# Four reorderings in a four-layer graph transformer: first weight between the first rows, expert loads prepared one ahead, first queries inside the graph stage, a token sum pinned

## The chip, the cores and the metric

The kernel runs on one core of one Trainium2 chip. The metric is the device time of one execution in microseconds, the median over several runs. Engines: PE (TensorE, matrix products and transposes), DVE (VectorE), ACT (ScalarE), POOL (GpSimd), and SP (SyncE), which issues most of the DMAs. Every engine works through its own instructions in a fixed order; an instruction that waits holds up all that stand behind it on that engine.

## The reference

The input is x with 1250 tokens of 512 features and 20,000 edges (src, dst) between tokens. Four layers follow each other, each of this form:

```python
xn = layernorm(x)
x = x + gnn(xn, edges) + mixer(xn)
x = x + ffn(layernorm(x))
```

What the change touches of them:

- Layer 0: the graph part is `relu` of a normalised neighbour sum of `xn @ W + b`; the mixer is a two-block performer attention, which begins with its own layer norm of xn with gain and bias, projects keys and values, and uses exponentials of `key @ projection` less half the key's squared norm.
- Layer 1: the graph part is `relu(batchnorm(mean_of_neighbours @ W_l + b_l + xn @ W_r))`; the mixer is a linear attention with a softmax over each query's features.
- Layer 2's feed-forward part: 8 experts, 2 per token, each `h1 = rmsnorm(gelu(x @ w1))`, `h2 = rmsnorm(gelu(h1 @ w2))`, output `(h1 + h2) @ w3`, summed with the gates' weights.
- Layer 3: the graph part is a `leaky_relu` of a normalised neighbour sum; the mixer is `mean(X @ Wv) + X @ kv / (n sqrt(d))` with `kv = (X @ Wtheta)^T (X @ Wv)`, where the mean is over all tokens.

## The kernel before, in words

The tokens lie in 10 tiles of 125 (NT = 10, TP = 125), the features in 4 chunks of 128 (NC = 4). `nat` tiles have tokens on partitions; `xnT` has features on partitions and all 1250 tokens in a row. Products are in float32 and pass through PE twice, so that one `mm` of four chunks over a 125-token tile is eight passes. Eight PSUM banks are handed out by `bank()`. Three weight buffers are handed out by `load_w` (L156), whose DMA goes on SP's queue. A planner in the framework (the tile scheduler) orders the instructions of each engine by their costs and dependencies, not by the order of the source; only what is wrapped in `tc.keep_in_program_order` keeps its place among the other wrapped instructions and what they stand behind.

*Opening, `layer0_mixers` and `l0_front`.* SP's queue starts with cols (per-feature biases and gains), then x in five loads of two tiles each, then the graph weight W. Per tile `ln_one` computes the layer norm on DVE (`bn_stats` L194, `bn_aggr` L196, a square root on ACT, a reciprocal L199, the scaling L200), z is a second normalisation of xn (L790), both are transposed on PE (L188); xn's transposed copy goes to xnTt by ACT, z's to `yT` (the same memory as `xnT`) with gain and bias from cols by DVE and ACT (L735). The product with W for tile t-1 stands in the source behind the preparation of tile t; its bias is added by DVE (L798) into hs.

*The graph's counting matrix, `Graph`.* In DRAM lies adj, 1250 x 1250 counts. `__init__` makes a tile of zeros out of x's last tiles (L555, DVE) and writes it over adj and a part of yd by DMAs on POOL's queue. `start` makes a key per edge, transposes the keys on PE (L584) and copies them (L585). `add` handles ten columns of edges: a load of the keys along a row (keyrow, two buffers, SP's queue), ten comparisons with every key (`same`, L614, DVE), then L617 and L618 on DVE and ten scatter-additions into adj by POOL (L620). There are 16 such groups, called between other work of layer 0.

*Layer 0's attention, `l0_attention`.* For one of four feature chunks `keys` runs the key projection (`proj_T`, three column blocks, evicted by DVE with bias into kT, L831), its square on ACT (L865), the squared sums on PE against `halves`, and then the products with the projection pj; `values` (L849) follow. At the end the output bias is added tile by tile to the residual (L1040, DVE, on `xm`, which is `xn` here).

*Layer 1.* `LinearAttention` (used as `att`) has `q_start`: a product with wq, a maximum (L1278), a subtraction (L1280), an exponential on ACT, a sum (L1285), a reciprocal (L1286) and a product (L1287). `out` calls it for the tiles 0 and 1, then per tile turns q (L188), starts the query two tiles on, and multiplies with `mix`. Ahead of it the graph part runs a loop over four features f (L1441 to L1452): eight products per column block, an Identity activation with bias into hT, batch statistics, a square root on ACT, four small DVE steps and a Relu with scale. hT is transposed back (L1462) tile by tile behind the attention's output.

*Layer 2's experts, `second` and `third`.* Sorted token rows are worked on in loads of one or two tiles of 128 rows. Per load, `second` loads w2, scales h1 by its root mean square (L1657, DVE) and transposes it (L1659, PE), evicts it with the gain n1 into h1T (L1702, DVE), multiplies with w2 and applies gelu on ACT (L1708). `third` does the same with h2 and n2, adds h1T (sT, L1724, DVE), multiplies with w3 and hands the result to `put`. Each load's chain stands in the source, and on PE, in this order: transposes, then products.

*Layer 3.* Each arriving tile of xn is transposed into xnT (ACT, L1772) and added to a Gram matrix (L1774). Then `graph(0)`, four products of the Gram matrix with wv whose results are copied into half (L145, by ACT and DVE in turn), the token sum tot over xnT (L1813, DVE), its spread totb (L1815, DVE), the product of totb with wv, whose result is added to x (`add_row` on POOL), and `graph(1)` follow, and then the products of half with wt.

Of the kernel before, what the change touches and what calls it, by code (L numbers as in the profile page):

```python
# [8 lines left out]
F32 = mybir.dt.float32  # L9
# [48 lines left out]
def gps_d4_kernel(ctx: ExitStack, tc: tile.TileContext, a: dict, out: bass.AP):  # L58
# [19 lines left out]
        for r in (slice(0, 112), slice(112, TP)):  # L78
            engine.dma_start(o[r], i[r])

    def load_x(engine, o):
        for t in range(0, NT, 2):
            move(engine, o[:, t:t + 2, :], a["x"][t * TP:(t + 2) * TP, :].rearrange("(t p) d -> p t d", p=TP))

    cols = const.tile([P, NCOL], F32, name="cols")
    nc.sync.dma_start(cols, a["cols"])
    ident = const.tile([P, P], F32, name="ident")
    make_identity(nc, ident)
    ones = const.tile([P, P], F32, name="ones")
# [98 lines left out]
            nc.tensor.transpose(ps[:, tok(c)], src[:, fea(c)], ident[:TP, :TP])  # L188
        return ps[:, :NC * TP].rearrange("p (c t) -> p c t", t=TP)

    def ln_one(o, src, t, between=lambda: None):

        st = S.small.tile([TP, 6], F32, tag="st1", name="st1", bufs=4)
        nc.vector.bn_stats(st, src[:, t, :])  # L194
        mv = S.small.tile([TP, 4], F32, tag="mv1", name="mv1", bufs=4)
        nc.vector.bn_aggr(mv[:, 0:2], st)  # L196
        nc.scalar.activation(mv[:, 2:3], mv[:, 1:2], AF.Sqrt, bias=eps5[:TP])
        between()
        nc.vector.reciprocal(mv[:, 2:3], mv[:, 2:3])  # L199
        nc.vector.tensor_scalar(o, src[:, t, :], mv[:, 0:1], mv[:, 2:3], op0=OP.subtract, op1=OP.mult)  # L200
        return mv
# [344 lines left out]
    class Graph:  # L546
# [1 line left out]

        def __init__(self, pool, first, x):
            self.pool = pool
            self.next = 0

            nc.vector.tensor_scalar(first, x[:, 7:, :].rearrange("p t d -> p (t d)")[:, :T], 3e38, 0.0,  # L555
                                    op0=OP.is_gt, op1=OP.is_lt)
            for t in range(NT):
                move(nc.gpsimd, adj[t * TP * T:(t + 1) * TP * T, :].rearrange("(p d) o -> p (d o)", d=T), first)
            nc.gpsimd.dma_start(adj[T * T:T * T + TP, :], first[:, 0:1])
            n = RARE * SL // 8  # L560
            for k in range(8):
                r = (NTI - RARE) * SL + k * n
                nc.gpsimd.dma_start(yd[r:r + n, :], first[:n, :D])
            self.count = pool.tile([TP, EC], F32, name="count")
            self.cell = pool.tile([TP, EC], I32, name="cell")

        def start(self, z):

# [202 lines left out]
                assert self.turned < self.rooted  # L771
                self.some()

    def l0_front(pool, x0, xn, hs):


        w = load_w(a["L0_gnn_W"])
        b = row_bc(a["L0_gnn_b"])
        yT = xnT
        before = None  # L780
        for t in range(NT + 1):
            if t < NT:
                mv = ln_one(xn[:, t, :], x0, t)
                r = S.small.tile([TP, 2], F32, tag="r2", name="r2", bufs=4)

                nc.vector.tensor_tensor(r[:, 0:1], mv[:, 2:3], mv[:, 2:3], op=OP.mult)
                nc.scalar.activation(r[:, 1:2], mv[:, 1:2], AF.Sqrt, bias=eps5[:TP], scale=r[:, 0:1])
                nc.vector.reciprocal(r[:, 1:2], r[:, 1:2])
                z = S.small.tile([TP, D], F32, tag="z", name="z")
                nc.vector.tensor_scalar(z, xn[:, t, :], r[:, 1:2], None, op0=OP.mult)  # L790
                xnTt = S.small.tile([P, NC, TP], F32, tag="xnTt", name="xnTt")
                nc.scalar.copy(xnTt, transposed(xn[:, t, :]))
                gained(yT, t, transposed(z), ("L0_mix_ln1_g", "L0_mix_ln1_b", 0))
            if before is not None:
                u, m = before
                ps = bank()
                mm(ps[:TP, :], [(m[:, c, :], w[:, c, :]) for c in range(NC)])
                nc.vector.tensor_tensor(hs[:, u, :], ps[:TP, :], b[:TP, :], op=OP.add)  # L798
            before = t, xnTt
        return yT, z  # L800

    def l0_gnn(rows, dis, hs, xn):
# [318 lines left out]
    def layer0_mixers():  # L1121
# [3 lines left out]
        with tc.tile_pool(name="l0a", bufs=1) as pool:  # L1125
            xn = nat(pool, "xn")
            hs = nat(pool, "hs")
            with tc.tile_pool(name="l0n", bufs=1) as lp:
                x0 = nat(lp, "x0")
                load_x(nc.sync, x0)  # L1130
                zero = lp.tile([TP, T], F32, name="zero")
                graph = Graph(gpool, zero, x0)
                yT, z = l0_front(pool, x0, xn, hs)
                graph.start(z)
            second = [Front(yT, xn, ("L0_mix_ln2_g", "L0_mix_ln2_b", 4 * i)) for i in range(2)]
            first = Front(yT, xn, ("L0_mix_ln1_g", "L0_mix_ln1_b", 4))
# [127 lines left out]
    class LinearAttention:  # L1264
# [22 lines left out]
            nc.vector.tensor_tensor(q, q, bc(m, C), op=OP.mult)  # L1287
            return q

        def out(self, pool, wq, use):  # L1290


            ready = [self.q_start(pool, t, wq) for t in range(2)]
            for t in range(NT):
                qT = pool.tile([P, NC, TP], F32, tag="qT", name="qT", bufs=3)
                nc.scalar.copy(qT, transposed(ready[t].rearrange("p h c -> p (h c)")))
                if t + 2 < NT:
                    ready.append(self.q_start(pool, t + 2, wq))
                ps = bank()
                mm(ps[:TP, :], [(qT[:, c, :], self.mix[:, c, :]) for c in range(NC)])  # L1300
                use(t, ps[:TP, :])
# [80 lines left out]
    def layer1_mixers():  # L1382
        scales = dram.tile([T, 1], F32, name="scales")
        with tc.tile_pool(name="l1x", bufs=1) as pool:
# [46 lines left out]
                add_to(mT[:, f, c0:c0 + cn], ps)  # L1431

            over(rows, False, more)
            hT = pool.tile([P, NC, T], F32, tag="n1", name="hT")
            for f in range(NC):
                st = S.small.tile([P, 5, 6], F32, tag="bst", name="bst")
                for c0, cn in CH:
                    ps = bank()
# [11 lines left out]
                nc.vector.tensor_tensor(g[:, 1:2], mv[:, 0:1], g[:, 0:1], op=OP.mult)  # L1450
                nc.vector.tensor_tensor(g[:, 1:2], col("L1_gnn_beta", f), g[:, 1:2], op=OP.subtract)
                nc.scalar.activation(hT[:, f, :], hT[:, f, :], AF.Relu, bias=g[:, 1:2], scale=g[:, 0:1])  # L1452
            rscope.close()

            b = row_bc(a["L1_mix_b_out"], late=True)
            ow = row_bc(a["L1_mix_out_norm_w"], late=True)
# [30 lines left out]
                return gT  # L1487

            arrival[1] = Arrival(1, a["L1_ffn_gw2"], hidden=hidden)
            with tc.tile_pool(name="l1o", bufs=1) as op:  # L1490
                att.out(op, wq, use)
                arrival[1].step(NT)

    def layer1_ffn():
        KH = 8
# [114 lines left out]
    def layer2_ffn():  # L1610
# [4 lines left out]
        with tc.tile_pool(name="l2o", bufs=1) as op:  # L1615
# [29 lines left out]
            with tc.tile_pool(name="l2e", bufs=1) as pool:  # L1645
# [16 lines left out]
                class Group:  # L1662
# [8 lines left out]
                    def first(self, source):  # L1671
# [15 lines left out]
                            o += n  # L1687
                        self.r1 = self.means(ss[:, :self.n], "r1")

                    def second(self):  # L1690
                        self.h1T = pool.tile([P, 2, GT * SL], F32, tag="h1T", name="h1T", bufs=2)
                        self.h2 = pool.tile([SL, GT, DH], F32, tag="h2", name="h2", bufs=2)
                        ss = pool.tile([SL, GT], F32, tag="s2", name="s2", bufs=2)
                        for i, (o, tiles) in zip(self.loads, self.at):
                            n = len(tiles)
                            e = expert(i)
                            w2 = op.tile([P, 2, DH], F32, tag="w2", name="w2", bufs=4)
                            nc.sync.dma_start(w2, a["L2_ffn_w2"][bass.ds(e, 1), :, :].rearrange("o (c p) h -> p (o c) h", p=P))
                            n1 = cols_of(e, "L2_ffn_n1", "n1")
                            pt = turned(self.h1, self.r1, o, n)  # L1700
                            for k in range(2):
                                nc.vector.tensor_scalar(self.h1T[:, k, o * SL:(o + n) * SL], pt[:, k, :], n1[:, k:k + 1], None,  # L1702
                                                        op0=OP.mult)
                            ps = bank()
                            for j in range(n):
                                mm(ps[:, j * DH:(j + 1) * DH],
                                   [(self.h1T[:, k, (o + j) * SL:(o + j + 1) * SL], w2[:, k, :]) for k in range(2)])
                            nc.scalar.activation(self.h2[:, o:o + n, :], ps[:, :n * DH].rearrange("p (j d) -> p j d", d=DH),  # L1708
                                                 AF.Gelu)
                            for j in range(o, o + n):  # L1710
                                square(self.h2[:, j, :], ss[:, j:j + 1])
                        self.r2 = self.means(ss[:, :self.n], "r2")

                    def third(self):
                        for i, (o, tiles) in zip(self.loads, self.at):
                            n = len(tiles)
                            e = expert(i)
                            w3 = half3().rearrange("p (c n) -> p c n", c=2)
# [4 lines left out]
                            for k in range(2):  # L1723
                                nc.vector.scalar_tensor_tensor(sT[:, k, :n * SL], pt[:, k, :], n2[:, k:k + 1],  # L1724
                                                               self.h1T[:, k, o * SL:(o + n) * SL], op0=OP.mult, op1=OP.add)
                            for j, t in enumerate(tiles):
                                ps = bank()
                                mm(ps, [(sT[:, k, j * SL:(j + 1) * SL], w3[:, k, :]) for k in range(2)])
                                put(pool, ps, t)

                def use(loads, source):
                    n = len(loads)
# [14 lines left out]
    def layer3_mixers():  # L1747

        with tc.tile_pool(name="l3a", bufs=1) as pool:
# [60 lines left out]
                copy(half[:, c, :], ps)  # L1810

            tot = S.small.tile([P, NC], F32, tag="tot", name="tot", bufs=1)
            nc.vector.tensor_reduce(tot, xnT, AX.X, OP.add)  # L1813
            totb = S.small.tile([P, NC, TP], F32, tag="totb", name="totb", bufs=1)
            nc.vector.tensor_scalar(totb, bc(tot, TP), 1.0 / T, None, op0=OP.mult)  # L1815
            ps = bank()
# [104 lines left out]
```

## Time and profile before

| | before |
|---|---|
| median of 9 runs | 3118.08 us (3110.11 to 3131.32) |
| the profiled execution | 3121.38 us |
| its span | 3119.4 us |
| mean granted clock of TensorE | 0.958 |
| DMA traffic | 275.69 MB, mean 88 GB/s |

The tables below are from that one execution; times are microseconds from the start of its span. A row of the timeline gives the start, the duration, engine, line, operation, what is written and read, the shape, the count of merged instructions, and in brackets the idle time of the engine ahead of it with what ended it ("<-DVE q L1287": VectorE's instruction on line 1287 that writes q). In such a row `x8` from a PE line are eight passes. "PEq" is PE's own instruction sequencer. The page's slices cut the span into 40 equal parts and give the busy share of each in tenths.

Busy time by stage (PE and DVE in us):

| stretch | length | PE | DVE | DMA share | granted clock | what it holds |
|---|---|---|---|---|---|---|
| 0 to 20 | 20.00 | 6.09 | 14.31 | 0.95 | 1.00 | loads, first layer norms |
| 20 to 61.5 | 41.50 | 41.50 | 19.84 | 0.86 | 1.00 | layer 0's product with W |
| 61.5 to 135 | 73.50 | 73.19 | 66.38 | 0.58 | 0.98 | layer 0's first key and value projections |
| 1726 to 1745 | 19.00 | 16.10 | 9.70 | 0.08 | 0.91 | layer 1's last batch norm, first queries |
| 2606 to 2718 | 112.00 | 94.75 | 49.67 | 0.50 | 1.00 | layer 2's experts, second and third products |
| 2786 to 2835 | 49.00 | 45.65 | 20.47 | 0.01 | 1.00 | layer 3's Gram matrix and token sum |

A granted clock below 1 in a stretch means that the throttle held PE at half speed for a part of it.

### The profile page before, as it was taken

The numbers are of one execution on the slowest core, as the hardware profiler recorded it, in microseconds if no ns is written. First come the engines' busy times: TensorE is split into PE (matmuls) and PEld (weight loads), VectorE is DVE, ScalarE is ACT, GpSimd is POOL, SyncE is SP. The second block draws the span as 40 slices with busy tenths as digits, with TensorE's granted clock in tenths as the row PEclk, the third lists the DMA queues.
The fourth block names the chain that finished last, engine by engine and source line by source line (L and its number), as shares of the span: only waits on it lengthen the run. The fifth ranks groups of instructions, "written<-read, shape, count | busy, mean of one in ns | idle before, by whom it ended". The sixth has DMA issues, their size and how long they took to land. (4 is left out here: it accounts for less than half of the span.)

```text
span 3119.4 us, 31412 instructions
## 1 busy us (share of the span) xinstructions
PE 2877.0 (92%) x11531; PEld 1720.4 (55%) x11531; DVE 1178.2 (38%) x2812; ACT 694.0 (22%) x1469; POOL 670.7 (22%) x492
## 2 busy tenths in 40 slices
PE   8999999999999999999899979999799979789884
PEld 4457744455576444655455546766454547345562
DVE  6835611143365423344531550001343135362433
ACT  3132311132333122111311431111241013230010
POOL 3444444442001300133310011000301002032023
PEclk9999999999999999999899989999899989999987
DMA  8411121121001200237310017775210026430096
GB/s 230 118 15 15 7 38 31 28 32 14 14 14 46 76 27 28 80 113 246 88 34 1 21 48 280 257 251 176 81 41 1 8 70 194 160 106 10 24 319 195
DMA packets 234381, 275.69 MB, mean 88 GB/s; under 512 B 104351, under 2 KB 131599, under 8 KB 234209
## 3 DMA queue, kind: packets, MB, share of 16 engines
q1 hardware_dynamic: 123841, 185.13, 18.5%
q0 software_dynamic: 96832, 63.67, 9.0%
q10 hardware_dynamic: 13536, 24.65, 2.1%
q8 instruction: 102, 1.67, 0.2%
q14 instruction: 70, 0.57, 0.1%
HBM read 228.04 MB, written 44.91 MB: 88 GB/s over the span
## 5 line engine op out<-in xcount | busy, mean ns | idle before, releaser
L182 PE MATMUL ps<-xnT,w 128*128 128x500 f32 (+1 forms) x1536 | 554.5, 515 | 2.8 <-PEq L698 2.2
L182 PE MATMUL ps<-w,hT 128*125 128x512 f32 (+1 forms) x1232 | 542.1, 592 | 0.7 <-ACT hT L1246 0.7
L182 PEld LDWEIGHTS ps<-xnT,w 128*128 128x128 f32 x1536 | 289.2, 190 | 251.8 <-issue 239.4
L620 POOL DMA_INDIRECT adj<-count,cell x160 | 318.3, 1990 | 369.0 <-DMA adj<-count,cell 345.7
L182 PEld LDWEIGHTS ps<-w,hT 128*125 128x125 f32 (+1 forms) x1232 | 228.8, 189 | 270.2 <-issue 261.1
L182 PE MATMUL ps<-w,xnT 128*125 128x512 f32 x560 | 254.7, 604 | 0.0
L182 PE MATMUL ps<-xgT,w 128*128 128x256 f32 (+1 forms) x1256 | 233.4, 344 | 2.8 <-issue 2.0
L182 PEld LDWEIGHTS ps<-xgT,w 128*128 128x128 f32 x1256 | 207.1, 193 | 43.3 <-issue 20.7
L378 POOL DMA_INDIRECT xg<-rows,r_idx x94 | 89.8, 955 | 571.1 <-PE ps L419 288.4
L208 DVE TENSOR_TENSOR xn<-ps,xn 125x512 f32<-125x512 f32 x100 | 69.0, 690 | 344.0 <-PE ps L182 344.0
L523 ACT ACTIVATE hT<-ps,cols 128x500 f32<-128x500 f32 (+1 forms) x108 | 65.6, 608 | 477.3 <-PE ps L182 477.3
L439 POOL DMA_INDIRECT came<-yd,slots x80 | 102.9, 1286 | 300.5 <-SPq L408 136.3
L182 PEld LDWEIGHTS ps<-w,xnT 128*125 128x125 f32 x560 | 103.6, 192 | 115.4 <-issue 115.0
L420 DVE COPY xgT<-ps 128x512 f32<-128x512 f32 x94 | 62.0, 687 | 246.3 <-PE ps L419 225.3
L182 PE MATMUL ps<-hs,AT 125*125 125x512 bf16 x600 | 132.6, 379 | 4.0 <-PEq L698 4.0
L182 PE MATMUL ps<-AT,n 125*128 125x500 bf16 (+1 forms) x720 | 127.2, 339 | 0.0
L429 DVE TENSOR_TENSOR y<-ps,erow 128x512 f32<-128x512 f32 x71 | 49.1, 692 | 194.4 <-PE ps L182 188.4
L182 PEld LDWEIGHTS <-AT 125*125 125x125 bf16 x600 | 81.3, 136 | 50.7 <-issue 6.1
L1532 ACT ACTIVATE hT<-ps,b 128x256 f32<-128x256 f32 (+1 forms) x112 | 48.8, 436 | 262.1 <-PE ps L182 262.1
L182 PEld LDWEIGHTS <-n 125*128 125x128 bf16 x720 | 70.0, 97 | 58.0 <-issue 1.1
L925 PE MATMUL ps<-ex,vw 125*65 125x256 f32 x320 | 83.6, 413 | 2.8 <-DVE vw L911 2.8
L208 DVE TENSOR_TENSOR x<-ps,x 125x512 f32<-125x512 f32 x50 | 34.5, 690 | 130.1 <-PE ps L182 116.8
(404 smaller groups left out, 3644.8 us busy)
## 6 DMA issues: line engine op xcount, KB each, us to landing
w<-in_L_ffn_we_dram SPq DMA_DIRECT2D x56, 1024.0 KB
w<-in_L_ffn_w_dram SPq DMA_DIRECT2D x58, 512.0 KB
yd<-y ACTq DMA_DIRECT2D x94, 256.0 KB
w<-in_L_mix_W_dram SPq DMA_DIRECT2D x16, 1024.0 KB
w<-in_L_ffn_w_dram SPq DMA_DIRECT2D x44, 256.0 KB
rows<-z SPq DMA_DIRECT2D x40, 224.0 KB
keyrow<-keys SPq DMA_DIRECT2D x16, 546.9 KB
erow<-in_L_ffn_b_dram SPq DMA_DIRECT2D x30, 256.0 KB
```

Source lines behind the costliest of these rows:

```text
L182: nc.tensor.matmul(o, l, r, start=(i == 0), stop=(i == n - 1))
L208: nc.vector.tensor_tensor(dst, ps, dst, op=OP.add)
L378: nc.gpsimd.indirect_dma_start(g, None, self.rows, bass.IndirectOffsetOnAxis(ap=self.idx[:, t:t + 1], axis=0))
L420: nc.vector.tensor_copy(xgT[:, :, j * SL:(j + 1) * SL], ps.rearrange("p (c s) -> p c s", c=NC))
L429: nc.vector.tensor_tensor(y, ps, bias, op=OP.add)
L439: nc.gpsimd.indirect_dma_start(y, None, yd, bass.IndirectOffsetOnAxis(ap=slots[n][:, k * NT + t:k * NT + t + 1], axis=0))
L523: nc.scalar.activation(hT[:, f, :cn], ps[:, :cn], act, bias=b1(f))
L620: nc.gpsimd.indirect_dma_start(adj, bass.IndirectOffsetOnAxis(ap=self.cell[:, c:c + 1], axis=0), self.count[:, c:c + 1], None, compute_op= ...
L925: nc.tensor.matmul(self.ps[j][:C + 1, :NB], self.vw[j][:, t, :], self.ex[k][:, j, u, :], start=(t == 0), stop=(t == NT - 1))
L1532: nc.scalar.activation(hT[f // NC][:, f % NC, :ns], ps[:, :ns], AF.Gelu, bias=b1[:, f:f + 1])
```

## The change

Four places, independent of each other:

1. Opening. x's first two tiles are loaded singly, W's load follows them, then tiles 2 and 3, then cols, then the rest of x. The zero fill and the clearing DMAs move out of `Graph.__init__` into `clear`, which `l0_front` calls at its seventh tile; the zero fill is pinned in program order, and so is the `bn_stats` of tile 2. The product with W lags two tiles behind the preparation instead of one, and xnTt has three buffers of a pool of its own.
2. Layer 2's experts. `second` and `third` are cut into `prepare` (weight load, scaling, transposes, eviction) and `use` (products and what follows), and a new method `ahead` issues the next load's `prepare` before this load's `use`.
3. Layer 1. The first two `q_start` calls are made ahead of the last of the four features of the batch-normed graph part; for that the attention's pool is opened, and the graph part's closed, before that loop.
4. Layer 3. The token sum's reduction is pinned in program order.

The diff, cut to its core:

```diff
-    def load_x(engine, o):
-        for t in range(0, NT, 2):
-            move(engine, o[:, t:t + 2, :], a["x"][t * TP:(t + 2) * TP, :].rearrange("(t p) d -> p t d", p=TP))
+    def load_x(engine, o, tiles=range(0, NT, 2), n=2):
+        for t in tiles:
+            move(engine, o[:, t:t + n, :], a["x"][t * TP:(t + n) * TP, :].rearrange("(t p) d -> p t d", p=TP))
...
-    nc.sync.dma_start(cols, a["cols"])
...
-    def ln_one(o, src, t, between=lambda: None):
+    def ln_one(o, src, t, between=lambda: None, in_order=False):
-        nc.vector.bn_stats(st, src[:, t, :])
+        ins = nc.vector.bn_stats(st, src[:, t, :])
+        if in_order:
+            tc.keep_in_program_order(ins)
...
-        def __init__(self, pool, first, x):
+        def __init__(self, pool):
...
-            nc.vector.tensor_scalar(first, x[:, 7:, :].rearrange("p t d -> p (t d)")[:, :T], 3e38, 0.0,
-                                    op0=OP.is_gt, op1=OP.is_lt)
+        def clear(self, first, x):
+            tc.keep_in_program_order(nc.vector.tensor_scalar(first, x[:, 7:, :].rearrange("p t d -> p (t d)")[:, :T], 3e38, 0.0,
+                                    op0=OP.is_gt, op1=OP.is_lt))
             for t in range(NT):
                 move(nc.gpsimd, adj[t * TP * T:(t + 1) * TP * T, :].rearrange("(p d) o -> p (d o)", d=T), first)
...
-    def l0_front(pool, x0, xn, hs):
-        w = load_w(a["L0_gnn_W"])
+    def l0_front(pool, x0, xn, hs, w, aside):
...
-        before = None
-        for t in range(NT + 1):
+        before = []
+        for t in range(NT + 2):
+            if t == 6:
+                aside()
             if t < NT:
-                mv = ln_one(xn[:, t, :], x0, t)
+                mv = ln_one(xn[:, t, :], x0, t, in_order=t == 2)
...
-                xnTt = S.small.tile([P, NC, TP], F32, tag="xnTt", name="xnTt")
+                xnTt = pool.tile([P, NC, TP], F32, tag="xnTt", name="xnTt", bufs=3)
...
-            if before is not None:
-                u, m = before
+            if t > 1:
+                u, m = before[t - 2]
...
-                load_x(nc.sync, x0)
+                load_x(nc.sync, x0, range(2), 1)
+                w = load_w(a["L0_gnn_W"])
+                load_x(nc.sync, x0, range(2, 4, 2))
+                nc.sync.dma_start(cols, a["cols"])
+                load_x(nc.sync, x0, range(4, NT, 2))
                 zero = lp.tile([TP, T], F32, name="zero")
-                graph = Graph(gpool, zero, x0)
-                yT, z = l0_front(pool, x0, xn, hs)
+                graph = Graph(gpool)
+                yT, z = l0_front(lp, x0, xn, hs, w, lambda: graph.clear(zero, x0))
...
-        def out(self, pool, wq, use):
-            ready = [self.q_start(pool, t, wq) for t in range(2)]
+        def first(self, pool, wq):
+            return [self.q_start(pool, t, wq) for t in range(2)]
+        def out(self, pool, wq, use, ready=None):
+            ready = ready or self.first(pool, wq)
...
             over(rows, False, more)
+            rscope.close()
+            oscope = ExitStack()
+            op = oscope.enter_context(tc.tile_pool(name="l1o", bufs=1))
             hT = pool.tile([P, NC, T], F32, tag="n1", name="hT")
             for f in range(NC):
+                if f + 1 == NC:
+                    ready = att.first(op, wq)
...
+                    def ahead(self, prepare, use):
+                        loads = [(i, *at) for i, at in zip(self.loads, self.at)]
+                        made = prepare(*loads[0])
+                        for k, load in enumerate(loads):
+                            now, made = made, prepare(*loads[k + 1]) if k + 1 < len(loads) else None
+                            use(*load, now)
...
-                        for i, (o, tiles) in zip(self.loads, self.at):
+                        def prepare(i, o, tiles):
...
+                            return w2
+                        def use(i, o, tiles, w2):
...
+                        self.ahead(prepare, use)
...
-            nc.vector.tensor_reduce(tot, xnT, AX.X, OP.add)
+            tc.keep_in_program_order(nc.vector.tensor_reduce(tot, xnT, AX.X, OP.add))
```

## The prediction

> **What bounds the kernel now.** I read the page from the top: the busy shares first, then the slices.
>
> ```profile
> PE 2877.0 (92%) x11531; PEld 1720.4 (55%) x11531; DVE 1178.2 (38%) x2812; ACT 694.0 (22%) x1469; POOL 670.7 (22%) x492
> ...
> PE   8999999999999999999899979999799979789884
> ...
> DVE  6835611143365423344531550001343135362433
> ```
>
> TensorE (PE) is busy 92% of the 3119.4 us span, in all stages but a few slices. So an edit is worth the PE idle time that it takes away or opens in its own stage, plus what the clock loses behind that idle time. I therefore went to the timeline of PE at the four places that the change touches, with VectorE (DVE) beside it. I also followed the order of instructions that the changed program has on each engine, because in all but the pinned places a scheduler decides that order.
>
> **The opening.** First PE, then DVE, before:
>
> ```profile
> 17.74 6.30 PE L182 MATMUL ps<-w,xnTt 128*125 128x512 f32 x8 [3.98 <-DMA w<-in_L_gnn_W_dram]
> ...
> 61.64 0.34 PE L584 MATMUL ps<-ident,kf 80*125 80x80 f32 x2
> 61.82 8.60 PE L182 MATMUL ps<-xnT,w 128*128 128x500 f32 x24
> 70.26 1.80 PE L182 MATMUL ps<-halves,sq 128*125 128x2 f32 x16
> ```
>
> ```profile
> 62.45 0.31 DVE L585 COPY key<-ps 125x160 f32<-125x160 f32 x1
> ...
> 63.02 0.34 DVE L614 SCALAR_TENSOR_TENSOR same<-keyrow,key,mask 125x125 f32<-125x125 f32 x1
> ...
> 65.71 0.74 DVE L831 TENSOR_SCALAR kT<-ps,cols 128x500 f32<-128x500 f32 x1
> ```
>
> PE waits 3.98 us for the first weight, then has no gap over 0.3 us until 135. The front end ends at 61.8 (call this E), the key projection takes 8.60, and at 70.26 the squared-key sums follow, which need kT by way of DVE's L831 and one ACT square (0.62 us).
>
> *Loads.* The weight now stands behind two tiles instead of ten. That could remove the 3.98 us, but two other things take its place. The changed PE order has the transposes of three tiles, not two, ahead of the first product. And DVE's four biased transposed copies (L735) of the first two tiles need cols, which landed at 2.95 and now stands behind 1 MB of x and the 1 MB weight. The x pairs (0.5 MB each) landed at 5.7, 7.77, 9.96, 12.21 and 14.69, so about 2.3 us per 0.5 MB: the 2 MB ahead of cols land at about 5.7 + 3 x 2.3 = 12.6, and cols at about 13. Tile 2's statistics, 0.53 + 0.48 of xn and z and its transposes (1.04 each, at the half clock) then end about 16 to 18.7. Against 17.74 that is -1.7 to +1; the 4.29 us per tile afterwards is PE's own. The zero fill (0.79 us) and the 42.8 us of clearing (18.63 to 61.45) start about 20 us later; the first scatter waits anyway, since POOL's first one had stood idle 242 us for x. I take **-0.3**.
>
> *What becomes late.* DVE is in order. Before, 10 comparisons (L614) stood between the key copy and the first kT eviction. In the changed order 60 do, with ten residual adds (L1040), five L617 and five L618. From start to start a comparison takes 0.27 us (63.28, 63.55, 63.83 in the trace), an add about 0.65 (0.68 long, starts 0.60 to 0.74 apart), an L617 and L618 together about 0.2. The first eviction then stands at 62.45 + 0.57 + 60 x 0.27 + 10 x 0.65 + 5 x 0.2 = 86.7 instead of 65.71: 21 us later. The projection's PSUM space suffices, so PE still ends it at E + 8.6; the sums start at 86.7 + 0.74 + 0.62 + 0.3 = 88.4, not 70.26. PE's order has nothing between: **18 us**, the lower end. The key rows come through two buffers by DMA, and the longest time from issue to use was 5.9 us (65.83 to 71.73). The first two groups of ten are loaded; four more at a round of (5.9 + 2.7)/2 = 4.3 end at 63.0 + 5.4 + 17.2 = 85.6 without the adds; the adds and the L617 and L618, if none lies in those waits, make it 93: 24 us. The late clearing shares the queues, hence an upper end of 26. I take **21**, and +1 (0 to 2) for a half-clock start behind the stall. Nothing is paid back: DVE's later load is smaller, but PE waited nowhere for it.
>
> **Layer 2's experts.** Between 2606 and 2718 PE has 28 gaps over 0.3 us, all of 0.44 to 1.05 us, 17.25 us together, of this kind:
>
> ```profile
> 2608.99 0.70 PE L182 MATMUL ps<-w,h1T 128*128 128x256 f32 x2 [0.58 <-DVE h1T L1702]
> ...
> 2688.05 3.70 PE L182 MATMUL ps<-w,sT 128*128 128x512 f32 x8 [0.58 <-DVE sT L1724]
> ```
>
> Each is four transposes, then DVE's normalising eviction (0.88 for two), then the product. The changed PE order puts the next load's transposes ahead of this load's products, whose 1.2 to 3.6 us cover the 0.88. What stays is the first load of each call (some four times 0.6) or, at worst, gaps where DVE's 1.66 us runs of L1657 stand ahead of the eviction (10 x 0.6). **-15** (-17 to -11).
>
> **Layer 1's queries.** Before:
>
> ```profile
> 1725.65 7.03 PE L182 MATMUL ps<-w,xnT 128*125 128x512 f32 x16
> 1735.58 0.62 PE L188 MATMUL ps<-ident,q 125*128 125x125 f32 x4 [2.90 <-DVE q L1287]
> 1736.03 5.30 PE L182 MATMUL ps<-w,xnT 128*125 128x512 f32 x8
> 1741.16 3.60 PE L182 MATMUL ps<-mix,qT 128*125 128x512 f32 x8
> ```
>
> PE waits 2.90 us for the softmax of the first queries, and then runs 5.30 for eight passes that take 3.60 two lines on: the granted clock was half until 1739.94. Moved ahead of the last feature's matmuls, the two softmaxes have some 20 us. New on the path is that feature's batch norm: 0.47 + 0.42 + 0.29, a table load of 1.28 (one of two that ACT gains), 0.29, four small DVE steps of 0.2 and a Relu of 1.43, together 5.0 to 5.4, against PE work of 0.43 + 3.43 + 3.43 = 7.3 before the first hT transpose. It is covered by 1.9; uncovered, a second table load would eat it. -2.90 - 1.7 = **-4.6** (-5 to -2.5).
>
> [...]
>
> **Layer 3's token sum.** Before, DVE then PE:
>
> ```profile
> 2794.03 5.36 DVE L1813 TENSOR_REDUCE tot<-xnT 128x4 f32<-128x5000 f32 x1 [1.00 <-ACT xnT L1772]
> ...
> 2826.70 0.69 DVE L145 COPY half<-ps 128x512 f32<-128x512 f32 x1 [6.17 <-PE ps L182]
> ```
>
> ```profile
> 2806.26 6.66 PE L182 MATMUL ps<-hs,AT 125*125 125x512 bf16 x30 [3.35 <-PEq L698]
> 2812.76 13.90 PE L182 MATMUL ps<-w,gram 128*128 128x512 f32 x32
> 2826.50 3.60 PE L182 MATMUL ps<-w,totb 128*125 128x512 f32 x8
> ```
>
> The sum's 5.36 us lay beside PE's products (2795.23 to 2802.26). Pinned, it stands in DVE's order behind both of its `half` copies, of which the second starts at 2826.70, 0.2 after the last `half` product. PE's order is unchanged: the totb product is next. The sum runs 2827.3 to 2832.7, totb (0.41) to 2833.1; PE waits 2833.2 - 2826.5 = 6.7 us, and 1.7 to 3.4 of half clock follow, as behind the 2.90 us above. Freed DVE time ahead could shorten the 3.35 us gap, but ACT's part of the chain ends last there: at most -1.2. **+8.9** (5.5 to 10).
>
> **Sum.** -0.3 + 21 + 1 - 15 - 4.6 + 8.9 = +11.0. On the profiled execution (3121.4 us, of which 3119.4 span) that is 3132.4. That run was 3.3 us over the median of the nine, so against the median: 3118.1 + 11 = **3129 us**. The lower ends give -1.7 + 18 - 17 - 5 + 5.5 = -0.2 (3118), the upper ones +1 + 26 + 2 - 11 - 2.5 + 10 = +25.5 (3144).
>
> **Rivals.**
>
> *The opening does not stall (faster).* The first kT eviction comes within 4 us of where it was, because the key copy and its comparisons get done beside the last products, or kT is taken in time some other way. DVE is busy for only 19.8 of the 41.5 us ahead of 61.5, which speaks for room; against it speaks that the key transposes stand on PE right before the projection in both orders, so no comparison can start earlier. Then 3129 - 22 = 3107; with the full -1.7 of the loads 3105. It decides below a stall of 4 us: there the total falls under 3112.
>
> *Layer 2's gaps stay*, since expert weights by DMA (share 0.50 in this stage) or ACT end last there: -15 becomes -3, the total 3141. Against it: 26 of the 28 gaps name DVE or ACT as what ended them, none a DMA.
>
> *The token sum is covered*, because PE finds it done (the pin leaves it ahead of a `half` copy): 3129 - 8.9 = 3120. Against it: the order itself.
>
> *The opening is worse*: key rows and the late clearing collide, DMA share being 0.95 in the first 20 us and 0.86 until 61.5. A stall of 29 or more gives 3138 and up.
>
> **Chances.** Forecast 0.56, split by its bounds into 0.48 slower and 0.08 within; no stall 0.15, faster; layer 2's gaps stay 0.10, slower; token sum covered 0.09, within; worse opening 0.10, slower. A measurement of this kernel tells about 0.2% from no change, which is 6.2 us. That makes faster 0.15, same 0.17, slower 0.68. The range leaves out most of the no-stall case and the ends of the two slow ones: 3110 to 3144.
>
> **What would show it.** Right: a PE gap of 17 to 26 us ended by DVE's kT (or ACT's square) ahead of the first squared-key sums; layer 2's experts with fewer than ten gaps; no gap before the first transpose of q; a gap of 6 to 7 us ended by totb. Wrong: PE dense between 60 and 100, or a DMA ending layer 2's gaps.

## The result and the profile after

The changed kernel takes 3130.27 us (median of 14 runs, 3123.11 to 3134.03) against 3120.21 us for the kernel before (45 runs): a ratio of 1.0033, 95% interval 1.0024 to 1.0042, or +10 us (7.5 to 13). The forecast was 3129, +11 against its reference. The profiled execution took 3132.04 us, its span is 3130.3 us, the mean granted clock 0.952 (before 0.958).

The page says little: PE's busy time is unchanged and the rest is idle time.

```profile
PE 2877.2 (92%) x11531; PEld 1725.3 (55%) x11531; DVE 1174.4 (38%) x2812; ACT 695.2 (22%) x1471; POOL 667.7 (21%) x492
...
PE   7799999999999999999799997999799998899884
```

The first two slices fell from 8 and 9 to 7 and 7; that is the opening. The timeline of PE there, and of DVE below it:

```profile
62.59 8.60 PE L181 MATMUL ps<-xnT,w 128*128 128x500 f32 x24
97.78 1.84 PE L181 MATMUL ps<-halves,sq 128*125 128x2 f32 x8 [26.58 <-ACT sq L869]
```

```profile
63.79 0.34 DVE L617 SCALAR_TENSOR_TENSOR same<-keyrow,key,mask 125x125 f32<-125x125 f32 x1
...
78.35 0.69 DVE L1044 TENSOR_TENSOR xn<-xn,row 125x512 f32<-125x512 f32 x1 [8.87 <-DMA row<-in_L_mix_bo_dram]
...
96.38 0.64 DVE L835 TENSOR_SCALAR kT<-ps,cols 128x500 f32<-128x500 f32 x1
```

PE waits 26.58 us ahead of the squared-key sums. The releaser named is ACT's square, but that only follows DVE's first kT eviction, which stands at 96.38 instead of 65.71. The middle DVE row says that 8.87 us of this were neither comparisons nor adds but a wait for the output bias (`row`). DVE waits for nothing else between the key copy (63.22) and that eviction; 60 comparisons and ten adds stand there, where before there were ten comparisons and no add.

Layer 2's experts, the second products of a group, on PE:

```profile
2632.69 0.82 PE L1674 MATMUL ps<-ident,h 128*128 128x128 f32 x6
2633.92 0.67 PE L181 MATMUL ps<-w,h1T 128*128 128x256 f32 x2 [0.41 <-ACT h L1697]
2634.42 0.27 PE L1674 MATMUL ps<-ident,h 128*128 128x128 f32 x1
2634.53 1.46 PE L181 MATMUL ps<-w,h1T 128*128 128x256 f32 x6
2635.83 0.49 PE L1674 MATMUL ps<-ident,h 128*128 128x128 f32 x3
```

Transposes and products now follow each other without a bracket. Of 28 gaps of over 0.3 us (17.25 us) four are left, the first of each call, 1.58 us together.

Layer 1, where q's transposes now follow the last feature directly (no bracket at 1764.69), and the next gap is 3.00 instead of 4.08. The first row is from before, the others are from the changed kernel:

```profile
1757.01 1.07 PE L188 MATMUL ps<-ident,z 125*128 125x125 f32 x4 [4.08 <-issue]
```

```profile
1763.01 1.85 PE L181 MATMUL ps<-mT,w 128*128 128x250 f32 x8
1764.69 0.59 PE L187 MATMUL ps<-ident,q 125*128 125x125 f32 x4
1765.12 3.60 PE L181 MATMUL ps<-w,xnT 128*125 128x512 f32 x8
...
1783.33 0.62 PE L187 MATMUL ps<-ident,z 125*128 125x125 f32 x4 [3.00 <-issue]
```

Layer 3, PE and then DVE:

```profile
2807.86 6.66 PE L181 MATMUL ps<-hs,AT 125*125 125x512 bf16 x30
...
2834.76 6.45 PE L181 MATMUL ps<-w,totb 128*125 128x512 f32 x8 [6.51 <-DVE totb L1852]
```

```profile
2828.29 0.69 DVE L144 COPY half<-ps 128x512 f32<-128x512 f32 x1 [6.17 <-PE ps L181]
2828.90 5.35 DVE L1850 TENSOR_REDUCE tot<-xnT 128x4 f32<-128x5000 f32 x1
2834.28 0.42 DVE L1852 TENSOR_SCALAR totb<-tot 128x500 f32<-128x500 f32 x1
```

The wait for totb is there, 6.51 us, and the product behind it takes 6.45 instead of 3.60. The first gather, however, has lost its gap of 3.35.

Where the time went, from how far the same PE instruction is later than before in the two profiled executions: +0.8 at the key projection (62.59 against 61.82), +29.9 at the value products (109.25 against 79.34), +25.5 at 220 us, +32.2 ahead of layer 1's last feature, +24.9 ahead of layer 2's experts, +4.7 behind them, +1.6 at layer 3's first gather, +11.1 behind the token sum. Between the opening and layer 1 the shift first falls by 5 us and then rises by 7, in parts that the change does not touch. Of the rise, 5 us are one place where the granted clock was 0.56 after and 1.00 before; the last section comes back to it.

### The profile page after: what moved, and what is told of

Its sections match the earlier page's. It is cut to its first block, busy times and chain, and to the rows that moved or that the text cites. A ratio compares the mean times of both kernels' runs of the same rounds, so it can differ in the third digit from the quotient of the medians.

```text
span 3130.3 us, 31423 instructions
## 1 busy us (share of the span) xinstructions
PE 2877.2 (92%) x11531; PEld 1725.3 (55%) x11531; DVE 1174.4 (38%) x2812; ACT 695.2 (22%) x1471; POOL 667.7 (21%) x492
```

## The experiments

Each was timed in several rounds beside runs of the kernel before on the same chip. Executions of one and the same kernel lie some 20 us apart, and their times follow the mean granted clock (kernel before: 3112 to 3117 us at 0.961, 3128 to 3131 at 0.955), which is why the stage's own rows are given beside each ratio.

**The four parts alone.** Each kernel is the kernel before with one of the four numbered parts of the change.

Opening: the first part of the diff, all of it.

> The kernel before with the first part of the change alone (loads, lag of two tiles, clearing moved). Theory (read from the changed kernel's trace): +26 us against before, from one PE gap of about 26 us ahead of the squared-key sums, the front end itself being 0.8 later and the half clock behind the gap adding 2 to 3. Rival (the prediction's terms): +21 to +22. Rival that the parts influence each other: under +15 alone. In the profile: the gap at the squared-key sums as in the changed kernel, about 26.6 us.

Measured: 1.0109 (1.0094 to 1.0123), +34 us (29 to 38). The gap, on PE, with the sums and what stands ahead:

```profile
61.91 8.60 PE L181 MATMUL ps<-xnT,w 128*128 128x500 f32 x24
96.22 1.84 PE L181 MATMUL ps<-halves,sq 128*125 128x2 f32 x8 [25.70 <-ACT sq L869]
```

The stall is this part's alone. All three expectations were too low for the timing. The rows say more than the gap: the value products behind it start at 107.70, first row below. Seven profiles have the opening of before (the kernel before and six of the runs below), and there these products start between 76.55 and 79.34, the latest being the kernel before, second row:

```profile
107.70 34.60 PE L181 MATMUL ps<-w,xnT 128*125 128x512 f32 x80
```

```profile
79.34 34.60 PE L182 MATMUL ps<-w,xnT 128*125 128x512 f32 x80
```

So the opening itself costs 28 to 31 us, which the interval holds at its lower end. What the timing has beyond that is not settled; the profiled execution, the lowest of the four (3144.59), lost only 23.5 us of span, since parts that the change does not touch ran some 5 us faster in it.

Experts: the `ahead` method with `prepare` and `use`.

> The kernel before with the second part alone (layer 2's loads prepared one ahead). Theory (trace of the changed kernel): -19 us, since each of the 28 removed gaps also costs PE a start of about 0.13 us that the gap's length does not count. Rival (the prediction's term): -15. Rival that the gaps only wandered elsewhere: -3 to +3. In the profile: PE gaps over 0.3 us between the second and third products under 2.5 us in all, instead of 17.25.

Measured: 0.9940 (0.9927 to 0.9952), -18.7 us (-15 to -23). The gaps between 2600 and 2702 fall to four, 1.58 us. The theory of -19 fits; -15 is just the interval's end, and the gaps' 15.7 lie inside it. The rows decide. The first transposes of h and the last product of the stage, before and then here:

```profile
2607.81 0.60 PE L1659 MATMUL ps<-ident,h 128*128 128x128 f32 x4
...
2717.03 3.67 PE L182 MATMUL ps<-w,sT 128*128 128x512 f32 x8 [0.62 <-ACT y L427]
```

```profile
2608.34 0.82 PE L1659 MATMUL ps<-ident,h 128*128 128x128 f32 x6
...
2693.41 7.03 PE L182 MATMUL ps<-w,sT 128*128 128x512 f32 x16
```

From 2607.81 to 2720.70 are 112.9 us, from 2608.34 to 2700.44 are 92.1: the stage is 20.8 us shorter, and as much in the changed kernel (2632.69 to 2724.80). Most of what it gained beyond the gaps can be read off two rows of the changed kernel above: without a wait the next row starts 0.16 ahead of the former's modelled end (2634.42 + 0.27 = 2634.69, next start 2634.53), with a wait it starts a whole gap behind it. 24 gaps fewer at 0.16 are 3.8, and 17.25 - 1.58 + 3.8 = 19.5.

Queries: `first`, called ahead of the last feature.

> The kernel before with the third part alone (layer 1's first queries ahead of the last feature). Theory (trace of the changed kernel): -6 to -8 us: the gap of 2.90, the half clock behind it (1.7), about 1.1 of the next gap of 4.08 and the half clock behind that one (1.7). Rival (the prediction's term): -4.6, with the next gap as before. Rival that the last feature's batch norm is uncovered: -2 or nothing.

Measured: 0.9985 (0.9975 to 0.9995), -4.7 us (-1.6 to -7.8). The interval holds the prediction's term, the theory's lower end and even the -2 of the uncovered batch norm; the trace decides. PE runs in it from the last feature to the hT transposes without a gap, so the batch norm is covered:

```profile
1727.98 0.59 PE L188 MATMUL ps<-ident,q 125*128 125x125 f32 x4
1728.41 3.60 PE L182 MATMUL ps<-w,xnT 128*125 128x512 f32 x8
...
1735.28 0.60 PE L1469 MATMUL ps<-ident,hT 128*125 128x128 f32 x4
...
1746.62 1.06 PE L188 MATMUL ps<-ident,z 125*128 125x125 f32 x4 [3.00 <-issue]
...
1748.31 5.68 PE L182 MATMUL ps<-w,xnT 128*125 128x512 f32 x8
```

The next gap is 3.00 instead of 4.08, as the theory says, but the product behind it took longer than before (5.68 against 4.46 there, at a granted clock of 0.81), which takes the 1.1 back. Over the whole stage, PE's rows move by -4.6 here, by -4.6 in the best version below, and by -7.5 in the changed kernel, where that product took 3.60 at a granted clock of 1.00. So the prediction's term is met in two of the three profiles, and the theory's -6 to -8 only in the one where the clock was full there.

Token sum: the pin alone.

> The kernel before with the fourth part alone (token sum pinned). Theory (trace of the changed kernel): +6.3 us: 6.5 of waiting for the totb product and 2.9 of half clock behind it, less 3.2 because the gap of 3.35 ahead of the first gather of the graph part is gone once the sum no longer stands ahead of the Gram copies on DVE. Rival (the prediction's term): +8.9, with that gap only 1.2 shorter. Rival that the gap's going in the changed kernel belongs to another part: +9.4 and a gap of 3.35 still there.

Measured: 1.0015 (1.0002 to 1.0029), +4.7 us (0.6 to 9.0), with these rows on PE:

```profile
2813.39 6.66 PE L182 MATMUL ps<-hs,AT 125*125 125x512 bf16 x30
...
2840.30 6.04 PE L182 MATMUL ps<-w,totb 128*125 128x512 f32 x8 [6.51 <-DVE totb L1815]
```

The gap ahead of the gather is gone here too, so its going belongs to the pin. In the stage: 6.51 + (6.04 - 3.60) - 3.2 = +5.8. The interval alone does not part 5.8 from 8.9; the rows do.

The four add up to +34 - 18.7 - 4.7 + 4.7 = +15, against +10 for all together; the four intervals in quadrature are about 8 wide either way, so they may well add up.

**What makes the stall.** Each of the next four kernels is the opening part alone, with the edit that is shown. In the changed order, 60 comparisons and ten adds stand ahead of kT. The tile `zero` lies in the pool that closes at the end of the front, and the attention's tiles are laid out behind it. The idea: one of them takes zero's memory, and so the scheduler holds DVE's fill of `v` (L841) and the first kT back behind the clearing DMAs that read zero. Taken apart:

```diff
-                zero = lp.tile([TP, T], F32, name="zero")
+                zero = gpool.tile([TP, T], F32, name="zero")
```

> The opening part alone, but the tile of zeros lies in the graph's own pool, so that no later tile of the attention takes its memory. Theory: the stall comes from the place of the zero tile; the attention's v and kT take its memory and so must stand behind the late clearing, which put 60 comparisons and ten residual adds ahead of kT on DVE. With the tile apart DVE's order around the first kT is that of before (10 comparisons ahead), the gap at the squared-key sums falls from 26 us to under 4, and the time is within -4 to +6 us of before. Rival (late DMAs: the clearing delays the output bias and the key rows, whatever the memory): a gap of 10 us or more stays, as the first comparisons wait for key rows; +10 to +20. Rival (front end: loads and lag): the gap is gone but the first product is still late, +1 to +3.

Measured: 1.0023 (1.0010 to 1.0035), +7 us (3 to 11). DVE's order around kT is that of before, ten comparisons and the first kT at 66.44, and the fill of v stands right behind the key copy, at 63.52 instead of 96.39. So the place of zero makes the order; which of the attention's tiles lies on its memory the traces do not show. But a second thing shows, DVE then PE:

```profile
66.44 0.74 DVE L835 TENSOR_SCALAR kT<-ps,cols 128x500 f32<-128x500 f32 x1
...
79.08 0.69 DVE L1044 TENSOR_TENSOR xn<-xn,row 125x512 f32<-125x512 f32 x1 [8.33 <-DMA row<-in_L_mix_bo_dram]
79.77 0.47 DVE L835 TENSOR_SCALAR kT<-ps,cols 128x250 f32<-128x250 f32 x1
```

```profile
70.99 1.80 PE L181 MATMUL ps<-halves,sq 128*125 128x2 f32 x16
...
80.82 1.00 PE L181 MATMUL ps<-halves,sq 128*125 128x2 f32 x4 [6.97 <-ACT sq L869]
```

One residual add stands ahead of the third kT eviction, and it waits for the bias, which is late here too. The gap of 6.97 lies between the theory (under 4) and its rival (10 or more), so both have a part in it: with the memory apart about 19 of the 26 us go, and 7 stay behind a late load.

The clearing moved forward, the zero tile where it was:

```diff
-            if t == 6:
+            if t == 0:
                 aside()
```

> The opening part alone, but with the clearing called at the first tile instead of the seventh; the zero tile lies where the attention's tiles follow it. Theory: the clearing ends some 10 to 20 us sooner, fewer comparisons (20) and adds (4) stand ahead of kT, which at 0.27 and 0.65 us each are 2.7 + 2.6 = 5 to 6 us more than before, so a gap of 3 to 8 us unless the output bias is late again; +3 to +9 us. Rival (DMA load): the bias load still waits for the clearing, a gap of 9 us or more. Rival (front end): the earlier zero fill and clearing slow the x loads and the first product comes 2 to 5 us later.

Measured: 1.0017 (1.0005 to 1.0028), +5.3 us (1.6 to 8.7).

```profile
62.49 8.60 PE L181 MATMUL ps<-xnT,w 128*128 128x500 f32 x24
73.41 1.03 PE L181 MATMUL ps<-halves,sq 128*125 128x2 f32 x8 [2.33 <-ACT sq L869]
```

A gap of 2.33 with the zero tile's memory still shared: clearing that ends sooner takes away both the bias wait (DVE waits for no load here) and most of the order, with 20 comparisons and four adds ahead of kT as the theory said. The whole stall therefore needs both, the shared memory and the late clearing. The key projection is at 62.49, against 61.91 to 63.11 in the four profiles with the late clearing, so the clearing does not set the front end.

The bias taken out of the way, with the zero tile and the late clearing as in the change:

```diff
+            bo = pool.tile([P, D], F32, tag="bo", name="bo")
+            src = a["L0_mix_bo"][i]
+            nc.sync.dma_start(bo, bass.AP(tensor=src.tensor, offset=src.offset, ap=[[0, P], [1, D]]))
             wk = load_w(a["L0_mix_Wk"][i])
...
-            bo = row_bc(a["L0_mix_bo"][i])
```

> The opening part as in the changed kernel (zero tile and late clearing as they are), but the output bias has a tile of its own and is loaded ahead of the key weight. DVE's order then has 60 comparisons and none of the ten adds ahead of kT. Theory: of the 26 us gap, the bias wait (8.9) and the adds (6.5) go, 10 to 12 us stay, all of it comparisons behind the memory of the zero tile; +11 to +16 us against before. Rival (the key rows): the comparisons meet late key rows in place of the bias, since the loads stand behind the same clearing; 16 us or more stay.

Measured: 1.0087 (1.0070 to 1.0103), +27 us (22 to 32). The theory falls and its rival holds, as the first row, DVE's, shows; the second is PE's.

```profile
81.74 0.35 DVE L617 SCALAR_TENSOR_TENSOR same<-keyrow,key,mask 125x125 f32<-125x125 f32 x1 [11.28 <-DMA keyrow<-keys]
```

```profile
96.91 1.84 PE L181 MATMUL ps<-halves,sq 128*125 128x2 f32 x8 [25.21 <-ACT sq L872]
```

With no bias to wait for and no adds ahead of kT, DVE waits 11.28 us for a row of keys instead. The bias was only the first load in the way. From 62 to 80 us the DMA engines are busy 0.94 of the time here and in the changed kernel, against 0.51 before and 0.48 with the clearing moved forward, and with the early clearing DVE waited for neither load. So it is the late clearing that holds up the loads DVE needs there.

All three mends together, with cols loaded first as before:

```diff
+    nc.sync.dma_start(cols, a["cols"])
...
-                nc.sync.dma_start(cols, a["cols"])
...
+                zero = gpool.tile([TP, T], F32, name="zero")
...
+            if t == 0:
                 aside()
```

> The opening part alone with three mends: the zero tile in the graph's pool, the clearing called at the first tile, and cols loaded first as before. Theory: both causes of the stall are gone (memory of the zero tile, and the output bias held up by the late clearing), so the gap at the squared-key sums is under 1 us; the first product starts some 2 to 4 us sooner than in the changed kernel, since tile 2's normalisation no longer stands on DVE behind copies that wait for cols; -3 to 0 us against before. Rival: the front end is bound by the x loads whatever cols does, and the key projection starts at 62.5 as in the changed kernel; +1. Rival: a gap of 2 us or more stays, from key rows or the bias.

Measured: 1.0001 (0.9988 to 1.0014).

```profile
60.91 8.60 PE L182 MATMUL ps<-xnT,w 128*128 128x500 f32 x24
69.35 1.80 PE L182 MATMUL ps<-halves,sq 128*125 128x2 f32 x16
```

The stall is gone, and the first product starts at 17.94 instead of the changed kernel's 19.83. The key projection is at 60.91, and at 60.13 in the second kernel with this opening (the last run below); with the opening of before it lies between 59.90 and 61.82 in seven profiles, so the earlier weight has brought nothing that shows. With cols late it lay between 61.91 and 63.11 in all five: about 2 us are what the late cols cost.

**A better place for the sum.** The pinned reduction, moved in the source behind `graph(0)`, ahead of the products of the Gram matrix:

```diff
             graph(0)
+            tot = S.small.tile([P, NC], F32, tag="tot", name="tot", bufs=1)
+            tc.keep_in_program_order(nc.vector.tensor_reduce(tot, xnT, AX.X, OP.add))
             for c in range(NC):
...
-            tot = S.small.tile([P, NC], F32, tag="tot", name="tot", bufs=1)
-            nc.vector.tensor_reduce(tot, xnT, AX.X, OP.add)
```

> The token sum alone changed: the same pinned reduction, but it stands in the source behind the first gather of the graph part and ahead of the products of the Gram matrix, so that DVE does it between that gather's three steps and its first copy of half, where it was idle for 4.66 us before. Theory: PE waits for neither totb nor the first gather; -3.2 us against before, since the gap of 3.35 goes and nothing follows. Rival: the sum delays DVE's first copy of half (by 0.7 us) and PE runs out of banks, a new gap of 1 us or more, -2 or less. Rival: the gap of 3.35 has another cause and stays: 0.

Measured: 0.9967 (0.9956 to 0.9978), -10 us. DVE, then PE:

```profile
2810.87 5.36 DVE L1808 TENSOR_REDUCE tot<-xnT 128x4 f32<-128x5000 f32 x1
2816.14 0.68 DVE L145 COPY half<-ps 128x512 f32<-128x512 f32 x1
```

```profile
2802.05 6.66 PE L182 MATMUL ps<-hs,AT 125*125 125x512 bf16 x30 [0.15 <-PEq L698]
...
2822.28 3.60 PE L182 MATMUL ps<-w,totb 128*125 128x512 f32 x8
```

Neither gap is there: 3.35 to 0.15, and no bracket at totb. That is 3.2 us; the timing said more, so it was timed again.

> The same kernel as in the run of the token sum right behind the first gather, timed again beside new runs of before. Its trace showed 3.2 us gained in its own stage, the timing 0.9967. Theory: the stage's 3.2 us are all there is and the rest was the half clock, which falls at free places elsewhere; 0.9985 to 0.9995. Rival: the 9 us are real and something outside the stage is faster: 0.996 to 0.9975 again.

Measured: 0.9983 (0.9969 to 0.9997), -5.3 us (-1 to -10). The 3.2 of the stage lie inside this interval, not inside the first one (-14 to -7). That the kernel is faster is shown; whether by more than its stage is open.

**The best version.** The experts' and the queries' parts and the sum in its new place, with the opening of before:

> The kernel before with the parts for layer 2's experts and layer 1's queries and the token sum right behind the first gather; the opening as before. Theory: the parts add up, -18.7 - 4.7 - 3.2 = -27 us, 3093. Rival: the half clock takes part of it back, since it falls at free places: -20.

Measured: 3084.78 us, 0.9874 (0.9859 to 0.9890), -39 us (-34 to -44). It beats both kernels. It is more than the expected -27, and the sum of the parts' first timings, -18.7 - 4.7 - 10 = -33.7, only comes up to the interval's end; with four executions, why is open. Its profiled execution (3093.4) is 28 us under that of before, as the rows of the parts say: -20.8 - 4.6 - 3.2 = -28.6. With the mended opening in place of that of before:

> The parts for layer 2 and layer 1, the token sum right behind the first gather, and the mended opening. Theory: the earlier combination with the opening as before was 0.9874 of before; with the mended opening 0 to 3 us less, 0.9865 to 0.988. Rival: the mended opening loses 1 to 5 us, 0.988 to 0.990.

Measured: 0.9900 (0.9881 to 0.9920). That is -31 us (-25 to -37), less than the theory's. The two intervals overlap, so nothing says that the mended opening helps, and the simpler version is the better choice.

## Why the prediction was right, point by point

The total was right (+11 forecast, +10 measured), and each of the four parts moved the way that was said. That the total came out this close is luck all the same: the losses of the opening (loads, stall, half clock) were put too low, and so was the gain of layer 2, while the loss of layer 3 was put too high; these errors cancelled.

- *Loads, -0.3 (-1.7 to +1).* The mechanism was right: DVE's copies wait for cols, first row, and PE waits for tile 2's xn behind them, second row.

```profile
12.82 0.72 DVE L738 TENSOR_SCALAR xnT<-ps,cols 128x125 f32<-128x125 f32 x2 [3.73 <-DMA cols<-in_cols_dram]
```

```profile
17.21 1.09 PE L187 MATMUL ps<-ident,xn 125*128 125x125 f32 x4 [6.25 <-DVE xn L201]
```

The size was not. The +0.8 of the two profiles lies inside the bounds only because the profile before is the latest of its seven: by the ranges given above, late cols make it about +2. The 1.04 of the transposes, called half clock there, stands beside a granted clock of 1.00 in the first 20 us before; in the changed kernel the transposes at 17.21 took 1.09 at a granted clock of 0.50. Nor was there much to gain. In four of the seven profiles the wait ahead of the first product is put down to ACT's square root (3.08 to 3.19 us) and not to the weight.
- *What becomes late, 21 (18 to 26).* Right mechanism, wrong size: 26.58 in the changed kernel, 25.70 alone. The count of instructions held: from the key copy to kT are 33.2 us (63.22 to 96.38), and without the wait of 8.87 that is 24.3, as the sum had it (62.45 to 86.7). The term that failed was the DMA wait, put down to the key rows at 0 to 6. DVE waited 8.87 us for the output bias, and with that taken away 11.28 for the key rows. The late clearing was named as a reason for the upper end and in a rival that got 0.10; the runs make it the cause of these waits. And the memory of the zero tile, which the prediction did not mention, is with the late clearing why the 60 comparisons stood there at all: with the tile apart the order is that of before.
- *Half clock behind the stall, +1.* 109.25 - 97.78 against 79.34 - 70.26 is 11.5 (granted clock 0.63) against 9.1 (0.81): 2.4, over the upper bound of 2.
- *Layer 2, -15.* The gaps went as said (17.25 to 1.58), but the stage is 20.8 shorter, more than the bound of -17. The term missed what a stop costs beside its gap: 5 us over 24 gaps, about 0.2 each.
- *Layer 1, -4.6.* Measured -4.7, and -4.6 in the rows of the part alone; the batch norm was covered, as argued. The 1.7 of half clock went with the gap of 2.90: the product behind q's first transposes takes 3.60 at a granted clock of 1.00 in the changed kernel, where it took 5.30 at 0.68 before.
- *Layer 3, +8.9.* The wait of 6.7 was 6.51 and the half clock behind it 2.85 (6.45 - 3.60, granted clock 0.57), both as said; of the 1.7 to 3.4, the 2.90 us gap shows the 1.7, and the 3.4 was the author's estimate. But the gap ahead of the gather was given "at most -1.2", since ACT's chain seemed to end last there; in the runs it fell by 3.2 to nothing. Before, DVE's reduction stood from 2794.03 to 2799.31 ahead of a step of the same chain (L675, at 2799.31) whose input from ACT was ready at 2795.0, so the true term is about +6.

Of the rivals, none came true. The worse opening came nearest, and its cause, the late clearing in the way of loads, is part of what the runs show; but the stall was 26.6 against the 29 that it asked for.

## What to carry to other kernels

With the late clearing reading a tile from the pool that closes next, the fill of `v` stood at 96.39; with that tile in a pool of its own it stood at 63.52. So where a transfer is made later, look for who inherits the source's memory, and what the scheduler then puts ahead of that. One late load held up DVE here for 8.87 us with the first kT eviction behind it, and taking that load out of the way only uncovered the next one behind the same traffic, for 11.28 us. A long reduction goes where its engine is idle, between two known rows (no wait for totb), rather than to the end of the list (6.51 us of it); and the short stops on the bounding engine were worth more than the sum of their gaps (20.8 us for 15.7).

## What the runs showed of the hardware that was not expected

The half clock did not follow from the length of the gap ahead of it here. The same gap of 2.15 us in layer 0, which the change does not touch, was followed by full speed before and by half speed after. Before:

```profile
928.69 0.62 PE L188 MATMUL ps<-ident,z 125*128 125x125 f32 x4 [2.15 <-DVE nb L998]
929.14 3.61 PE L182 MATMUL ps<-cx,qfT 128*125 128x65 f32 x32
932.59 3.65 PE L182 MATMUL ps<-w,oT 128*125 128x512 f32 x8
```

After:

```profile
955.21 0.62 PE L187 MATMUL ps<-ident,z 125*128 125x125 f32 x4 [2.15 <-DVE nb L1002]
955.66 6.35 PE L181 MATMUL ps<-cx,qfT 128*125 128x65 f32 x32
961.81 5.94 PE L181 MATMUL ps<-w,oT 128*125 128x512 f32 x8
```

6.35 + 5.94 against 3.61 + 3.65 is 5 us from one place that nobody changed. The granted clock was 1.00 from 928.5 to 938.5 before and 0.56 from 955 to 965 after. The two traces say more. In both, every stretch of half or of full clock but the last is a whole multiple of 3.413 us, the shortest of them (3.41 of half clock from 1736.53 before, 10.24 from 956.17 after). Counted on in such steps, the gap lies whole between two of these times in the changed kernel: it lasts from 953.06 to 955.21, between 952.76 and 956.17, and the half clock comes at the second of them, for 10.24 us. Before, such a time, 927.57, falls inside the gap (926.54 to 928.69), with 1.12 us of the gap behind it, and the clock stayed at 1.00. So 2.15 us of idle time was enough once and not enough another time, and where the gap fell differed between the two; that this decides is the author's estimate from one case of each, and what exactly is counted is not shown. For reading a comparison it means that 5 us between two single profiles may be nothing but this, and that a stage's own rows have to be asked before a total is believed.
